# Filtered columns for five of six row components of a 3x3 convolution, with two sums moved from VectorE to accumulating DMAs

## The chip, the cores and the metric

One core of a Trainium2 chip runs the whole kernel. A core has TensorE (PE: matrix products; weight loads are its own row, PEld), VectorE (DVE), ScalarE (ACT), GpSimd (POOL) and SyncE (SP, which only issues transfers), with sixteen DMA engines. Each engine works through its own instructions in order, and engines wait for one another by semaphores. The metric is the device time of one launch in microseconds (us), as the median of several runs.

## The reference, cut to what matters

Two bottleneck blocks follow each other on an input x of 4 x 1024 x 56 x 56, all in float32. Layer 0 is a block with a deformable 3x3 convolution; layer 1 is a plain one with batch norms:

```python
out = relu(bn(conv(x, w1, b1), g1, be1))          # 1x1, 1024 -> 256
out = relu(bn(conv(out, w2, b2, pad=1), g2, be2)) # 3x3, 256 -> 256
out = bn(conv(out, w3, b3), g3, be3)              # 1x1, 256 -> 1024
out = relu(x + softplus(residual_scale)[0] * out)
```

`bn` takes the mean and the variance of each channel over all images and pixels. So nothing can be normalised before the whole convolution in front of it is done, and the kernel falls into stages at these points. The change lies in the 3x3 convolution of layer 1 and in what prepares and reads it. Its output before the batch norm is called y2.

## The kernel before, in words

**Stages.** Layer 0 runs from the start to about 2064 us. It also computes the first 1x1 convolution of layer 1 and stores that (y1) to DRAM. Then comes the 3x3 stage of layer 1 (to about 2378 us), a stage of second moments that gives the statistics of the last batch norm without computing its input (to about 2470 us), and the last stage, which computes the 1x1 convolution to 1024 channels, adds x and stores the output.

**The 3x3 stage.** An image of 56 rows is cut into two halves of 28 rows, so there are eight parts (`parts`). Within a part four output rows at a time are computed from six row components, p = 0 to 5, a fast convolution with four outputs along the rows; a part has QUADS = 7 such groups of four rows. Filters are transformed to the six components beforehand (`filters`, in layer 0), inputs are transformed on VectorE (`inputs`, lines 1150 to 1195), and the six products are turned back into four rows on VectorE (`end`, lines 1295 to 1333). The components are taken in the order `SEQ` = 1, 2, 3, 4, 0, 5. Each is first written into one of the four rows of its output (`TARGET`): components 0 and 1 into row class 0, component 2 into class 1, 3 into class 2, 4 and 5 into class 3.

Within a component, the three taps along a row are handled in one of two ways. Components in `WIN` have *filtered columns*: two neighbouring output columns come from four products (in `begin` one that goes to odd columns with the factor -2, in `middle` one that is added and copied to the even columns, in `end` one added to the odd and one subtracted from the even columns). The other components have five terms for a pair of columns. A term is 2 x 2 products of 128 x 128 filters (input and output channels are in two blocks of 128 each, `KB` = 2), with 7 x 28 = 196 columns, or 7 x 29 = 203 for one of the five. All go through `products`, line 1224.

For a filtered component ScalarE copies the odd columns out of the accumulator q (line 1238), and TensorE must wait for this copy before `middle` adds to q; then ScalarE copies the even columns (line 1262), and TensorE must wait for that before `end` adds to q again. The fourth product goes to a bank b of its own, and VectorE subtracts it (line 1278). Filters of filtered components need sums over the taps, `column_filters` (lines 772 to 781): components 2 and 4 get them in layer 0 (`EARLY`), component 5 at the start of the 3x3 stage (line 1401).

**Around the products.** `load(i)` brings the y1 rows of a part from DRAM into the place of the last image of y2 and ScalarE normalises them into the buffer d (line 1141). For a second half the row above it comes by a small transfer of its own into `edge`. `passes(i)` (line 1351) lets ScalarE read the finished rows of a middle part and sum values and squares for the batch norm: eight passes of 784 elements, two to each step of the loop. The first and last part (`ENDS`) use VectorE's statistics instead (line 1293).

**Order of the work.** The loop at line 1403 is written so that a component's `begin` stands ahead of the previous component's `end` and its own `middle` behind. A planner in the framework then orders the instructions of each engine by its own estimate of their times, so the order on the chip is near to, not equal to, that of the program. The transforms back of component 4 (`outer` and `inner`, lines 1303 to 1311) must be done before ScalarE may write component 5's odd columns, since both are in row class 3.

**Layer 0's filters.** `filters` (line 705) is a generator; the loop over the taps of the last image calls it once a tap. It loads the filters of layer 1, transforms them on VectorE, stores those of component 0 and their tap sum (`us_0`, in a buffer of the tag x1t that layer 0's last products also use) to DRAM, since their place is needed for the first rows of y1, and loads these.

**Reading y2.** y2 lies in SBUF, one tile for each image, rows in their order. The stage of moments reads it in runs of 128 pixels, the last stage in blocks of eight rows (`wide` line 1456, `sums_of_input` line 1637).

Of the kernel before, what the change touches and what calls it, by code (L numbers as in the profile page):

```python
# [8 lines left out]
F32 = mybir.dt.float32  # L9
# [22 lines left out]
WIN = (2, 4, 5)  # L32
EARLY = (2, 4)
# [28 lines left out]
def deform_bottleneck_then_bn_bottleneck(  # L62
# [27 lines left out]
    u0_d = dram.tile([128, KB * 3 * CB], F32, tag="u0_d", name="u0_d")  # L90
    y1_d = dram.tile([N, CB, HW], F32, tag="y1_d", name="y1_d")
# [81 lines left out]
    with ExitStack() as l0:  # L173
# [531 lines left out]
        def filters():  # L705
# [30 lines left out]
            def times(factor):  # L736
# [15 lines left out]
            nc.sync.dma_start(u0_d, w_0)  # L752
            us_0 = w3p.tile([128, 512], F32, tag="x1t", name="us_0", bufs=X1S)
            w_00 = w_0.rearrange("p (h j o) -> p h j o", h=KB, j=3)
            nc.vector.tensor_add(
                us_0.rearrange("p (h o) -> p h o", h=KB), w_00[:, :, 0], w_00[:, :, 1]
            )
            nc.sync.dma_start(us0_d, us_0)
            yield
# [7 lines left out]
            for p in (1, 3):  # L767
                us[p] = pool.tile([128, KB, CB], F32, tag=f"us{p}", name=f"us{p}")
                nc.vector.tensor_add(us[p], u[p][:, :, 0], u[p][:, :, 1])
                yield  # L770
# [12 lines left out]
        def raw_rows(to, n, half):  # L783

            lo = HALF * half
            for h in range(KB):
                nc.sync.dma_start(
                    to[:, h].rearrange("p r w -> p (r w)"),
                    y1_v[n, :, h, lo * W : (lo + HALF + 1 - half) * W],
                )  # L790
# [281 lines left out]

    with l1:
# [19 lines left out]
        nc.sync.dma_start(u[5], b_w2.rearrange("(h p) (i j) o -> i p h j o", p=128, j=3)[2])  # L1093
        for p in range(6):
            if p not in us:
                us[p] = wino.tile([128, KB, CB], F32, tag=f"us{p}", name=f"us{p}")
        nc.sync.dma_start(us[0], us0_d.rearrange("p (h o) -> p h o", h=KB))
        sum_t = wino.tile([128, KB, QUADS, W], F32, tag="sum_t", name="sum_t")
# [15 lines left out]
        edge = wino.tile([128, KB, W], F32, tag="edge", name="edge")  # L1114

        def load(i):

            n, half = parts[i]
            d = next_d if i else first_d
            pieces = []  # L1120
            if i == 0:
                for h in range(KB):
                    pieces.append((d[:, 1:, h, :], rows_t[:, h, : HALF + 1, :], h))
            else:
                lo = HALF * half
                land = y2[N - 1].rearrange("p h (r w) -> p h r w", w=W)[
                    :, :, lo : lo + HALF + 1 - half
                ]
                if half:
                    nc.sync.dma_start(edge, y1_v[n, :, :, (lo - 1) * W : lo * W])  # L1130
                raw_rows(land, n, half)
                for h in range(KB):
                    if half:
                        pieces.append((d[:, 0, h, :], edge[:, h], h))
                    pieces.append((d[:, 1 : 1 + HALF + 1 - half, h, :], land[:, h], h))
            nc.gpsimd.memset(d[:, HALF + 1 if half else 0], 0.0)
            for to, of, h in pieces:

                for e in range(2):
                    c = slice(e * (W // 2), (e + 1) * (W // 2))  # L1140
                    nc.scalar.activation(
                        to[..., c],
                        of[..., 1 - e : W : 2],
                        AF.Relu,
                        bias=sh1[:, h : h + 1],
                        scale=sc1[:, h : h + 1],
                    )
            return d

        def inputs(i, d, ps):  # L1150
# [5 lines left out]
            for hs in [slice(h, h + 1) for h in range(KB)] if i == 0 else [slice(0, KB)]:  # L1156
# [46 lines left out]
        def rows_of(n, half, r):  # L1203

            t = y2[n].rearrange("p o (r w) -> p o r w", w=W)
            r0 = HALF * half + r
            return t[:, :, r0 : r0 + 4 * (QUADS - 1) + 1 : 4, :]
# [10 lines left out]
        def products(ps, terms, first=False, last=False, alone=False):  # L1218

            for o in range(KB):  # L1220
                of = slice(o * 128, (o + 1) * 128)
                pairs = [(wt[:, h, of], x[:, :, h]) for h in range(KB) for wt, x in terms]
                for j, (wt, x) in enumerate(pairs):
                    nc.tensor.matmul(  # L1224
                        ps[:, o].rearrange("p r c -> p (r c)"),
                        wt,
                        x,
                        start=first and j == 0 and (alone or o == 0),
                        stop=last and j == len(pairs) - 1,
                        skip_group_check=not alone,  # L1230
                    )

        def begin(i, p):
# [13 lines left out]
            products(b, [(u[p][:, :, 1], x0)], first=True, last=True, alone=True)  # L1247
# [9 lines left out]

        def middle(i, p, q):
            if p in WIN:
                even, _ = halves(i, p)  # L1260
                products(q, [(u[p][:, :, 1], vs[p][..., :half_w])])
                nc.scalar.copy(even, q)

        def end(i, p, q):
# [7 lines left out]
            if p in WIN:  # L1272
                x0, x1 = v[p][..., :half_w], v[p][..., PW // 2 : PW // 2 + half_w]
                products(q, [(u[p][:, :, 2], x1)], last=True)
                b = bank(psb, "b", i, p, half_w)
                products(b, [(u[p][:, :, 0], x0)], first=True, last=True, alone=True)
                nc.vector.tensor_add(odd, odd, q)
                nc.vector.tensor_sub(even, even, b)
# [19 lines left out]
            elif p == 4:  # L1298
# [3 lines left out]

                def outer():
                    for o in range(KB):
                        stt(r[2][:, o], far_t[:, o], 4.0, sum_t[:, o], ALU.mult, ALU.add)
                    nc.vector.tensor_add(sum_t, sum_t, far_t)

                def inner(far):
                    for o in range(KB):
                        stt(far[:, o], r[3][:, o], 8.0, r[1][:, o], ALU.mult, ALU.add)  # L1310
                        stt(r[1][:, o], r[3][:, o], 2.0, r[1][:, o], ALU.mult, ALU.add)

                if i < len(parts) - 1:
                    outer()
                    inner(far_t)
                else:
                    inner(last_far)
# [4 lines left out]
            elif p == 0:  # L1322
                nc.vector.tensor_add(r[0], r[0], sum_t)
# [7 lines left out]
            elif p == 5:  # L1331
                nc.vector.tensor_add(r[3], r[3], far_t)
# [6 lines left out]
        CUTS = 2  # L1339
# [11 lines left out]
        def passes(i):  # L1351
            n, half = parts[i]
            size = HALF * W // CUTS
            for o in range(KB):
                for c in range(CUTS):
                    at = half * HALF * W + c * size
                    k = (i - 1) * CUTS + c
                    for f, func in enumerate((AF.Identity, AF.Square)):
                        nc.scalar.activation(
                            passed,  # L1360
                            y2[n][:, o, at : at + size],
# [34 lines left out]
        for ps in ((1, 2), (3, 4), (0,), (5,)):  # L1396
            inputs(0, ds[0], ps)
            for p in ps:
                if p in WIN and p not in EARLY:
                    for _ in column_filters(p):  # L1400
                        pass
        before, passing = None, iter(())
        for i, p in [(i, p) for i in range(len(parts)) for p in SEQ] + [(len(parts), None)]:
            begun = begin(i, p) if p is not None else None
            if before is not None:
# [9 lines left out]
                for _ in range(2):  # L1415
# [40 lines left out]
    def wide(n, j, k, name):  # L1456
        pz = ps1.tile([128, BLK], F32, tag="bank", name=f"{name}_{n}_{j}_{k}")
        for h in range(KB):
# [3 lines left out]
                y2[n][:, h, j * BLK : (j + 1) * BLK],  # L1462
# [174 lines left out]
    def sums_of_input(two):  # L1637

        (b11, b21), (b12, b22) = (
            [y2[n][:, h, j * BLK : (j + 1) * BLK] for h in range(KB)] for n, j in two  # L1640
# [3 lines left out]
        sub(t[:, 0], b12, b11)  # L1644
        sub(t[:, 1], b22, t[:, 0])
        sub(t[:, 2], b22, b12)
        sub(t[:, 3], b21, t[:, 1])
# [145 lines left out]
```

## Time and profile before

| | before |
|---|---|
| median of 3 runs | 2800.26 us (2799.1 to 2804.15) |
| the profiled execution | 2796.42 us, span 2794.6 us |
| granted TensorE clock, mean | 0.992 |
| line 1224 (all products of the 3x3 stage) | 1728 records, first at 2071.8, last ends at about 2372.4 us |
| line 1359 (statistics passes), ScalarE | 48 of 948 ns, and 48 of 187 ns that read the sum |
| line 1141 (normalising the rows), ScalarE | 32 of about 1.1 us, 16 of 0.4 us for the edge rows |
| POOL gathers of layer 0, line 509 | 900 of 1225 ns |

The page gives for each engine its busy time and share of the span, a chain of the work that ended last, and groups of instructions by source line. A line such as "L1238 ACT" is line 1238 of the kernel on ScalarE; "out<-in" names tiles. A table of stretches gives, for a window of time, each engine's busy time and number of instructions, then the granted clock, DMA share and GB/s.

### The profile page before, as it was taken

The numbers are of one execution on the slowest core, as the hardware profiler recorded it, in microseconds if no ns is written. First come the engines' busy times: TensorE is split into PE (matmuls) and PEld (weight loads), VectorE is DVE, ScalarE is ACT, GpSimd is POOL, SyncE is SP. The second block draws the span as 40 slices with busy tenths as digits, with TensorE's granted clock in tenths as the row PEclk, the third lists the DMA queues.
The fourth block names the chain that finished last, engine by engine and source line by source line (L and its number), as shares of the span: only waits on it lengthen the run. The fifth ranks groups of instructions, "written<-read, shape, count | busy, mean of one in ns | idle before, by whom it ended". The sixth has DMA issues, their size and how long they took to land.

```text
span 2794.6 us, 39694 instructions
## 1 busy us (share of the span) xinstructions
PE 2723.3 (97%) x12045; PEld 1928.1 (69%) x12045; DVE 2185.8 (78%) x5199; ACT 1496.3 (54%) x3045; POOL 1176.1 (42%) x1054
## 2 busy tenths in 40 slices
PE   9979999999999999999999999999989999999999
PEld 7655666776666676677667667667769999864554
DVE  5488887888788788877788888988759988337777
ACT  2345655575555655555565666666643444524444
POOL 0166554566655456556555656654500000111111
PEclk9999999999999999999999999999999999999999
DMA  8689999999999989999998999999831110219998
GB/s 286 200 300 368 389 324 339 328 349 339 341 335 363 349 296 317 328 351 348 352 349 269 362 370 333 340 343 375 268 123 31 42 39 9 95 53 343 349 346 303
DMA packets 313318, 792.70 MB, mean 284 GB/s; under 512 B 33768, under 2 KB 134672, under 8 KB 313104
## 3 DMA queue, kind: packets, MB, share of 16 engines
q0 software_dynamic: 127296, 462.48, 46.3%
q1 hardware_dynamic: 167376, 276.30, 28.7%
q10 hardware_dynamic: 18432, 51.39, 4.7%
q8 instruction: 95, 1.56, 0.2%
q14 instruction: 119, 0.97, 0.1%
HBM read 640.94 MB, written 143.75 MB: 281 GB/s over the span
## 4 chain that ended last, share of the span: by engine, by line
PE 81%; DMA 6%; DVE 6%; ACT 3%; issue 3%; SPq 1%; ACTq 0%; POOLq 0%; DVEq 0%
PE acc L574 20%; PE acc L662 11%; PE pr L636 10%; PE acc L331 8%; PE q L1224 6%; PE stp L546 6%; PE u L1674 3%; DMA g<-table,idxs 3%; PE acc_g L1506 2%; DVE s L521 2%; PE c L1674 2%; PE v L1674 2%; PE pm L421 2%; PE b L1224 2%; PE acc L868 1%
## 5 line engine op out<-in xcount | busy, mean ns | idle before, releaser
L509 POOL DMA_INDIRECT g<-table,idxs x900 | 1102.8, 1225 | 912.3 <-DVE s L521 244.3
L521 DVE SCALAR_TENSOR_TENSOR s<-g,wts,s 128x256 f32<-128x256 f32 (+1 forms) x2700 | 1173.4, 476 | 270.0 <-ACT s L519 130.0
L574 PE MATMUL acc<-sts,w 128*128 128x256 f32 (+2 forms) x3528 | 721.0, 355 | 2.8 <-ACT sts L552 1.4
L574 PEld LDWEIGHTS acc<-sts,w 128*128 128x128 f32 x3528 | 601.8, 190 | 54.1 <-ACT sts L552 4.3
L519 ACT ACTIVATE s<-g,wts 128x256 f32<-128x256 f32 x900 | 425.3, 511 | 213.7 <-PE stp L546 87.6
L636 PE MATMUL pr<-r,w 128*128 128x512 f32 (+2 forms) x896 | 365.8, 545 | 7.4 <-ACT r L609 4.0
L662 PE MATMUL acc<-x1t,c1w 128*128 128x512 f32 (+2 forms) x896 | 357.4, 541 | 7.5 <-ACT acc L283 4.2
L546 PEld LDWEIGHTS stp<-ident,s 128*128 128x128 f32 (+1 forms) x1800 | 211.5, 141 | 133.5 <-issue 92.0
L331 PE MATMUL acc<-xt,w 128*128 128x448 f32 x704 | 283.1, 544 | 6.7 <-DMA xt<-in_x_dram 6.7
L662 PEld LDWEIGHTS acc<-x1t,c1w 128*128 128x128 f32 x896 | 167.3, 190 | 146.6 <-issue 93.3
L636 PEld LDWEIGHTS pr<-r,w 128*128 128x128 f32 x896 | 165.0, 192 | 139.5 <-issue 84.3
L546 PE MATMUL stp<-ident,s 128*128 128x128 f32 (+1 forms) x1800 | 249.0, 273 | 10.2 <-DVE s L521 6.5
L552 ACT COPY sts<-stp 128x512 f32<-128x512 f32 (+2 forms) x504 | 241.1, 528 | 21.3 <-PE stp L546 21.0
L647 ACT ACTIVATE x1t<-pr,ch 128x512 f32<-128x512 f32 (+2 forms) x224 | 141.8, 633 | 139.8 <-PE pr L636 117.1
L331 PEld LDWEIGHTS acc<-xt,w 128*128 128x128 f32 x704 | 131.8, 192 | 111.1 <-issue 108.5
L1625 ACT ACTIVATE x1f<-x1f,sh_bn 128x896 f32<-128x896 f32 x112 | 116.0, 1041 | 150.2 <-DVE x1f L1622 129.6
L672 ACT COPY y<-acc 128x512 f32<-128x512 f32 (+2 forms) x112 | 59.5, 531 | 223.7 <-PE acc L662 212.1
L556 DVE TENSOR_TENSOR sts<-sts 128x512 f32<-128x512 f32 (+2 forms) x252 | 155.1, 615 | 0.8
L632 ACT COPY pr<-xr 128x512 f32<-128x512 f32 (+2 forms) x224 | 121.5, 542 | 3.8
L1622 DVE SCALAR_TENSOR_TENSOR x1f<-u,sc_bn,x1f 128x448 f32<-128x448 f32 x156 | 106.6, 683 | 18.9 <-PE u L1674 9.4
L1224 PE MATMUL q<-v,u 128*128 128x196 f32 x576 | 109.8, 338 | 8.4 <-DVE v L1176 7.7
L554 DVE TENSOR_TENSOR sts<-sts 128x256 f32<-128x256 f32 (+2 forms) x252 | 97.2, 386 | 23.4 <-ACT sts L552 22.0
(298 smaller groups left out, 3053.8 us busy)
## 6 DMA issues: line engine op xcount, KB each, us to landing
xt<-in_x_dram SPq DMA_DIRECT2D x112, 448.0 KB
x1f<-x_d SPq DMA_DIRECT2D x96, 448.0 KB
out_dram<-x1f ACTq DMA_DIRECT2D x96, 448.0 KB
xr<-in_x_dram SPq DMA_DIRECT2D x128, 256.0 KB
x_d<-x1t SPq DMA_DIRECT2D x128, 256.0 KB
table<-ft SPq DMA_DIRECT2D x56, 384.0 KB
g<-table,idxs POOLq DMA_INDIRECT x900
xr<-in_x_dram SPq DMA_DIRECT2D x64, 192.0 KB
```

Of the source, the lines that this page charges most:

```text
L331: nc.tensor.matmul(acc, w1[:, k, h * 128 : (h + 1) * 128], xts[n, j, k - k % 2][:, k % 2, :], start=start, stop=(k == KC - 1), skip_group_ ...
L509: nc.gpsimd.indirect_dma_start(out=g[:m], out_offset=None, in_=tables[n].rearrange("r q c -> r (q c)"), in_offset=bass.IndirectOffsetOnAxi ...
L519: nc.scalar.activation(s[:m], g[:m, 0:CB], AF.Copy, scale=wt[:, 0])
L521: nc.vector.scalar_tensor_tensor(s[:m], g[:m, corner * CB : (corner + 1) * CB], wt[:, corner], s[:m], ALU.mult, ALU.add,)
L546: nc.tensor.transpose(banks[h][:, t * 128 : t * 128 + m], s[:m, h * 128 : (h + 1) * 128], ident[:m, :m],)
L552: nc.scalar.copy(to, banks[h][:, :size].rearrange("p (e q) -> p e q", e=2))
L556: nc.vector.tensor_sub(sts[:, 5:7, :half], sts[:, 1:4:2, :half], sts[:, 0:2, :half])
L574: nc.tensor.matmul(sums[i], w2[:, a, k], sts[:, b, :half], start=(k == 0 and i % 2 == 0), stop=(k == TAPS - 1), skip_group_check=True,)
L636: nc.tensor.matmul(z, w3[:, h, k * 128 : (k + 1) * 128], r2[:, h, :size], start=False, stop=(h == KB - 1), skip_group_check=True,)
L662: nc.tensor.matmul(z, c1w[:, k, h * 128 : (h + 1) * 128], x1ts[k], start=False, stop=(i == KC // 2 - 1), skip_group_check=True,)
L1224: nc.tensor.matmul(ps[:, o].rearrange("p r c -> p (r c)"), wt, x, start=first and j == 0 and (alone or o == 0), stop=last and j == len(pai ...
L1674: nc.tensor.matmul(to, wt, x, start=start, stop=stop, skip_group_check=True)
```

## The change

- `WIN` becomes (0, 2, 3, 4, 5): components 0 and 3 get filtered columns too. `EARLY` becomes (2, 3, 4).
- In the middle parts (and in the last, but for its component 5) the even columns of a filtered component go another way. In `middle` ScalarE writes -q into a fresh bank b (a *seed*) instead of copying q to the even columns; in `end` TensorE adds the fourth product onto this bank, and ScalarE writes -b to the even columns. VectorE has no subtraction there.
- y2 is stored by row class: within an image, rows 0, 4, 8, ... come first, then rows 1, 5, 9, ..., and so on (`classes`). The four rows of a part are then contiguous, and VectorE's sums in the transform back take both channel blocks in one instruction (`joined`). Readers that need eight rows in order use `block_rows`.
- The two last sums of a middle part (row class 0 plus `sum_t`, row class 3 plus `far_t`) are transfers that add to their target, issued by GpSimd (`onto`); in the first and last part VectorE still does them.
- Statistics passes are cut by row class: sixteen of 392 elements a part, three to a step.
- The row above a second half is loaded together with its rows; `edge` goes.
- The tap sums of the filters of component 5 move to layer 0, with those of components 0 and 3, and go through DRAM as component 0's do (`u5_d`, `us5_d`).
- In part 0 only the inputs of components 1 and 2 are done one channel block at a time.

```diff
-WIN = (2, 4, 5)
-EARLY = (2, 4)
+WIN = (0, 2, 3, 4, 5)
+EARLY = (2, 3, 4)
...
-            nc.sync.dma_start(u0_d, w_0)
-            us_0 = w3p.tile([128, 512], F32, tag="x1t", name="us_0", bufs=X1S)
...
-            nc.sync.dma_start(us0_d, us_0)
-            yield
+            for p, w_p, u_d, us_d in ((0, w_0, u0_d, us0_d), (5, w_2, u5_d, us5_d)):
+                us_p = w3p.tile([128, 512], F32, tag="x1t", name=f"us_{p}", bufs=X1S)
+                u[p] = w_p.rearrange("p (h j o) -> p h j o", h=KB, j=3)
+                us[p] = us_p.rearrange("p (h o) -> p h o", h=KB)
+                yield from column_filters(p)
+                nc.sync.dma_start(u_d, w_p)
+                nc.sync.dma_start(us_d, us_p)
+                yield
...
+    def classes(t):
+        return t.rearrange("p o (c q w) -> p o c q w", c=4, w=W)
+
+    def block_rows(n, h, j):
+        return classes(y2[n])[:, h, :, 2 * j : 2 * j + 2, :].rearrange("p c q w -> p q c w")
...
-            for hs in [slice(h, h + 1) for h in range(KB)] if i == 0 else [slice(0, KB)]:
+            by_h = (i, ps) == (0, (1, 2))
+            for hs in [slice(h, h + 1) for h in range(KB)] if by_h else [slice(0, KB)]:
...
         def rows_of(n, half, r):
-            t = y2[n].rearrange("p o (r w) -> p o r w", w=W)
-            r0 = HALF * half + r
-            return t[:, :, r0 : r0 + 4 * (QUADS - 1) + 1 : 4, :]
+            return classes(y2[n])[:, :, r, QUADS * half : QUADS * (half + 1), :]
...
+        def seeded(i, p):
+            return i > 0 and (i, p) != (len(parts) - 1, SEQ[-1])
+
         def middle(i, p, q):
             if p in WIN:
                 even, _ = halves(i, p)
                 products(q, [(u[p][:, :, 1], vs[p][..., :half_w])])
-                nc.scalar.copy(even, q)
+                if seeded(i, p):
+                    seeds[i, p] = bank(psb, "b", i, p, half_w)
+                    nc.scalar.activation(seeds[i, p], q, AF.Copy, scale=-1.0)
+                else:
+                    nc.scalar.copy(even, q)
+
+        def onto(i, to, t):
+            if i in ENDS:
+                nc.vector.tensor_add(to, to, t)
+            else:
+                nc.gpsimd.dma_start(to, t, accum_op=ALU.add)
...
                 products(q, [(u[p][:, :, 2], x1)], last=True)
-                b = bank(psb, "b", i, p, half_w)
-                products(b, [(u[p][:, :, 0], x0)], first=True, last=True, alone=True)
-                nc.vector.tensor_add(odd, odd, q)
-                nc.vector.tensor_sub(even, even, b)
+                if seeded(i, p):
+                    b = seeds.pop((i, p))
+                    products(b, [(u[p][:, :, 0], x0)], last=True)
+                    nc.vector.tensor_add(odd, odd, q)
+                    nc.scalar.activation(even, b, AF.Copy, scale=-1.0)
+                else:
...
                 def outer():
-                    for o in range(KB):
-                        stt(r[2][:, o], far_t[:, o], 4.0, sum_t[:, o], ALU.mult, ALU.add)
-                    nc.vector.tensor_add(sum_t, sum_t, far_t)
+                    stt(r2, f_t, 4.0, s_t, ALU.mult, ALU.add)
+                    nc.vector.tensor_add(s_t, s_t, f_t)
...
-                    inner(far_t)
+                    inner()
+                    stt(f_t, r3, 6.0, r1, ALU.mult, ALU.add)
...
-                nc.vector.tensor_add(r[0], r[0], sum_t)
+                onto(i, joined(r[0]), joined(sum_t))
...
-                nc.vector.tensor_add(r[3], r[3], far_t)
+                onto(i, joined(r[3]), joined(far_t))
...
-        CUTS = 2
+        CUTS = 4
...
-                for _ in range(2):
+                for _ in range(3):
                     next(passing, None)
...
-                y2[n][:, h, j * BLK : (j + 1) * BLK],
+                block_rows(n, h, j),
```

## The prediction

> **What bounds the kernel now.** I read the page first, then the table of stretches, the groups by line and the waits of the 3x3 stage, its chain of waits, and last the timeline around one row component.
>
> ```profile
> span 2794.6 us, 39694 instructions
> PE 2723.3 (97%) x12045; PEld 1928.1 (69%) x12045; DVE 2185.8 (78%) x5199; ACT 1496.3 (54%) x3045; POOL 1176.1 (42%) x1054
> ```
>
> TensorE is busy for 97% of the span, so work taken off it can count, wherever no other engine sets the pace. The change is in the 3x3 stage of layer 1, from about 2072 to 2374 us. The stretches of that stage (columns: length, then busy time and instructions of PE, weight loads, VectorE, ScalarE, GpSimd, then clock, DMA share, GB/s):
>
> ```profile
> 2072.00:2160.00 88.00, 87.81 (x502) 86.80 (x503) 86.90 (x156) 26.74 (x52) 1.12 (x8) 0.97 0.16 58
> 2160.00:2350.00 190.00, 189.18 (x1102) 184.80 (x1102) 166.86 (x251) 96.75 (x188) 2.61 (x19) 1.00 0.11 36
> ```
>
> Two things are to be seen. TensorE is full in both. VectorE is full too up to 2160 (86.9 of 88 us), and after that has 12% left (166.9 of 190). ScalarE has half its time left, DMA nearly all. A part (half an image, eight in all) now takes 300.4 us (first to last product, 2071.8 to 2372.2) / 8 = 37.6 us.
>
> What a product costs, from the chain of waits in one part (start, length, engine, tile, line, records; each 128x128 product leaves two records):
>
> ```profile
> 2210.28 1.38 PE b L1224 x8
> 2211.65 1.36 PE q L1224 x8
> ```
>
> Four products of 203 columns take 1.38 us, four of 196 take 1.36 or 1.34. From the timeline of part 0, VectorE as TensorE comes to row 5's second product (line 1311 is the last operation that row 5's first copy waits for):
>
> ```profile
> 2111.36 1.02 DVE L1310 SCALAR_TENSOR_TENSOR far_t<-y 128x392 f32<-128x392 f32 x2
> 2112.30 1.03 DVE L1311 SCALAR_TENSOR_TENSOR y<-y 128x392 f32<-128x392 f32 x2
> 2113.26 1.02 DVE L1293 BATCH_NORM_STATS2 y_stats<-y 128x6 f32<-128x392 f32 x2
> 2114.20 0.95 DVE L1177 SCALAR_TENSOR_TENSOR v<-vs,v 128x784 f32<-128x784 f32 x1
> ```
>
> Starts that follow without a gap give the cadence: 0.885 us for 784 elements, 0.475 for 392.
>
> And ScalarE's hand on TensorE, from the queries on line 1262 (the first three) and line 1238 (the last two): who waited for these copies, us and times:
>
> ```profile
>   PEld q L1224: 4.2, 13
>   DVE y L1278: 1.0, 3
>   PE q L1224: 0.5, 2
>   PEld q L1224: 1.8, 6
>   PE q L1224: 0.2, 1
> ```
>
> **The change, part by part.**
>
> *Products.* A row without filtered columns has five terms, 20 products a part (4 of them 203 wide); one with them has four, 16 products of 196. Rows 0 and 3 change over: 2 rows x 8 parts x 1.38 us = **-22.1 us** on TensorE. A part goes from 37.6 to about 34.8 us.
>
> *VectorE, middle parts* (1 to 6). Inputs: rows 0 and 3 trade one 406-element operation (0.49) for two of 392 and one of 784 (1.835): +1.345 each, +2.69. Begin and end: rows 0 and 3 go from two 392-element operations to one, rows 2, 4, 5 also from two to one, because ScalarE now subtracts: 5 x -0.475 = -2.38. The joined sums: three pairs of 392 become three of 784, 3 x -0.065 = -0.2. The two sums that become DMAs: -1.77. Net -1.65 on 166.86/190 x 37.6 = 33.0, so 31.4 us for 34.8 us of TensorE. VectorE stays second there, at 90%.
>
> *VectorE, start and part 0*, where it is already full. Stage start: row 5's filter sums leave (cadence 0.60 + 0.60 + 0.33 + 0.60 = -2.1), rows 3 and 4 done whole +0.6, row 0 +1.1, row 5 -0.4: -0.8. Part 0 has neither seeds nor DMAs: +2.69 - 0.2 = +2.5. So VectorE reaches line 1311 of part 0 where it does now, about 2113, while TensorE has 2 x 1.38 us less to do before it; part 1 repeats this. What TensorE saves in parts 0 and 1, 2 x 2.76 = 5.5 us, is therefore not had: **+5.5**. The ends: +2 if TensorE runs further ahead into part 1 while row 5 waits (it has 8 products of row 1 to fill with), +9 if VectorE's extra 2.5 us comes on top.
>
> *ScalarE.* A filtered row now takes three ScalarE steps (odd columns, seed, even columns; 0.41 us each by cadence) instead of two, in five rows instead of three. Two of them stop TensorE: the odd copy before the second product, the seed before the third and fourth. Before, the fourth was free to be put anywhere; now it waits for its seed. Today's 48 copies hold the weight loads up 6.0 us and the products 0.7. For 80 such copies: 6.0 x 80/48 = 10.0, **+4.0**. Ends: 0.7 x 80/48 = 1.2, +0.5 (loads run ahead of the products, so not all of it reaches them); three steps in five rows, 6.0 x 120/48 = 15, +9. The statistics passes go from 8 of 0.95 + 0.19 us to 16 of about 0.53 + 0.19, some 2 us more a part; the edge copies (4 x 0.4 us on every other part) go. ScalarE comes to some 21 of 34.8 us, but in order: behind a pass that waits stand the next row's odd copy and seed, and for these waits TensorE.
>
> *The two DMAs a part* (12 in all). Each is issued by POOL behind ScalarE's even and VectorE's odd columns. Behind it on POOL stands only the clearing of one column of v (0.12 us), for which VectorE's difference waits. The profile has no transfer within SBUF, nor an adding one. The nearest row for the issue is line 509, 1225 ns a gather, so 1.2 us; for the data the first hardware queue: 28.7% of 16 x 2794.6 us over 167,376 packets is 77 ns for a packet of 1.65 KB. Here 256 runs of 1568 B over 16 engines: 16 x 77 ns = 1.2 us, doubled for reading the target, 2.5 us. The Trainium skill ("DMA: Bandwidth & Descriptors", anatomy of one DMA) states a fixed 2.0 us besides bytes over 436 GB/s; with 401 KB that is an estimated 2.9, and with the issue 4.1. Row and fixed part together: 1.2 + 2.5 + 2 = 5.7 us. The first pass comes after the second product of row 5, row 1's twelve and row 5's last eight: 24 x 0.34 = 8.2 us, and the pass over row 3's class is the seventh, two row steps later. So **0**, hidden behind 8.2 us of products; without that cover 5.7 us of ScalarE twice a part.
>
> A rule that speaks against it: the same skill's "SBUF — State Buffer" (section "two separate sides", the "DVE blocks DMA" trap) says that POOL, writing descriptors, is shut out of a port pair that certain VectorE operations hold for their whole length. The row is line 509, which ran beside a VectorE 78% busy at 1.2 us mean, up to about 3 us in the timeline. By the row the sum is unchanged; by the rule, at 3 us, landing is 7.5 us, still inside 8.2 but with nothing left. I go by the row and keep the rule for the slow rival.
>
> *Layer 0.* Ten more small VectorE operations (0.6 or 0.33 us, 5.4 in all) and two stores (1.0 MB, at 350 GB/s 3 us of DMA) while the gathers hold DMA above 90%; SP issues the first rows' load behind them, which ran at 1899 us, needed at 2066, so it has room. The second sum tile takes one of six x1t buffers for a few taps. TensorE is full there and has other blocks' work to turn to: **+2**, between 0 and 6.
>
> *Tail and last stage.* In part 7 the end is VectorE's (line 1299 at 2364.0 to the statistics at 2377), so row 0's saving there, 1.38, is lost; one 0.475 operation and a little more go: **+0.8**. Products on the blocks of 8 rows read four runs of 56; line 1224 reads runs of 28 at full rate, so 0. GpSimd's four differences (1.14 us each) have 20 us of products over them.
>
> Sum: -22.1 + 5.5 + 4.0 + 0 + 2 + 0.8 = **-9.8 us**. The profiled execution took 2796.4 (span 2794.6 and 1.8 around it), 3.8 below the median of the runs, 2800.3. So 2786.6 for a profiled one, and **2790** on the scale of the median.
>
> **Rivals.**
>
> *Everything fills up.* The order of TensorE's work is planned, and now loses under 1 us in 190. With +2, +0.5 and 0 for layer 0: -22.1 + 2 + 0.5 + 0.8 = -18.8, 2781. For it: the spare 12% of VectorE. Against: VectorE at 99% to 2160.
>
> *Saving eaten on the spot.* VectorE +9, ScalarE +9, layer 0 +2, tail 0.8: -1.3, 2799. For it: ScalarE already runs 7 us without a gap (passes between line 1141's copies, 2270 to 2277) and TensorE waited there.
>
> *Slower: passes stuck behind the adding DMA.* If landing takes longer than the 8.2 us of cover, ScalarE stands still in front of a pass, odd copy and seed behind it, and TensorE has some 4 products (1.4 us) in hand. Each part then loses landing less 9.6. It takes 9.8 + 5.6 = 15.4 us over six parts, 2.6 each, to be slower: a landing of 12.2 us. At 15 us: 6 x 5.4 = 32, 2822. For it: gathers of up to 11.4 us stand in the chain of layer 0. Against: these are under a DMA share of 0.9 and more, here it is 0.11.
>
> **How the numbers follow.** Forecast 0.42 (2785 to 2794); everything fills 0.17; eaten 0.18; slower 0.23. 0.2% is 5.6 us, about what a measurement here tells from no change. Faster 0.58, same 0.18, slower 0.24. The range leaves out the best tail and most of the slow rival's upper half: 2779 to 2812.
>
> **What would show it.** Right: 1600 records of line 1224 instead of 1728, from first to last about 288 us; VectorE full until some 2150 with TensorE gaps only there; passes that start without waiting on a DMA. Wrong: TensorE gaps in every part, before products that wait on the seed or odd copy (then ScalarE was mis-sized), or with a pass waiting for the DMA ahead of them (then the landing).

## The result, and the profile after

The changed kernel takes 2814.69 us (median of 12 runs, 2803.99 to 2820.12) beside 2798.45 us for the kernel before (12 runs, 2794.54 to 2804.15): ratio 1.0051, 95% interval 1.0037 to 1.0066. It is slower by some 14 us by the ratio (16 between the two medians), where 2790 was forecast; the range given ended at 2812. Run again beside later experiments it came to 1.0048 (1.0030 to 1.0067).

The profiled execution took 2820.12 us, at the top of those 12; another, 12 us shorter, has the same 3x3 stage (313.0 and 314.4 us). So only the stage is compared below, and not the spans. First the page of the kernel after:

```profile
span 2818.0 us, 39650 instructions
PE 2716.3 (96%) x11917; PEld 1912.8 (68%) x11917; DVE 2182.4 (77%) x5152; ACT 1520.3 (54%) x3159; POOL 1192.4 (42%) x1080
```

TensorE has 128 records of products fewer (11917 for 12045), as the change says, and lower busy time, yet the span grew. So TensorE waits somewhere. The table of stretches of the kernel after, with windows that answer to the two shown of before (this stage starts 6 us later here), the whole stage, and 8 us of part 0 (columns as before: length, then busy time of PE, weight loads, VectorE, ScalarE, GpSimd, then clock, DMA share, GB/s):

```profile
2078.00:2166.00 88.00, 82.17 (x454) 80.20 (x455) 83.68 (x129) 24.09 (x45) 2.74 (x12) 0.94 0.19 65
2166.00:2356.00 190.00, 172.64 (x979) 164.79 (x979) 157.18 (x215) 112.52 (x270) 15.99 (x39) 0.99 0.23 56
...
2077.90:2390.90 313.00, 285.14 (x1600) 273.00 (x1600) 261.05 (x374) 155.83 (x366) 20.22 (x56) 0.98 0.20 54
...
2122.00:2130.00 8.00, 6.41 (x20) 5.89 (x21) 8.00 (x14) 1.79 (x5) 0.19 (x1) 0.57 0.01 2
```

The same stage of the kernel before:

```profile
2071.80:2372.20 300.40, 299.24 (x1731) 293.38 (x1732) 269.00 (x437) 132.62 (x259) 3.90 (x30) 0.99 0.12 40
```

Before, TensorE was busy for 299.2 of 300.4 us of this stage. Now it is busy for 285.1 of 313.0: it lost 1.2 us to idling then and loses 27.9 now, along the whole stage, while no other engine is full after 2166 (VectorE 83%, ScalarE 59%). Waits set the pace there, and not an amount of work.

The chain of waits of the kernel after, where part 2 goes over into part 3, shows two of them (start, length, engine or transfer, tile, line):

```profile
2196.04 0.48 DVE y L1296
...
2197.06 4.38 DMA y<-sum_t
...
2201.46 0.03 ACT y L1254
...
2202.85 0.39 ACT y L1297
2203.24 0.60 ACT passed L1385 x2
2203.84 0.18 issue
2204.02 4.40 DMA y<-far_t
...
2208.54 0.58 DVE y L1309
2209.12 0.04 issue
2209.17 5.12 PE q L1227 x28
2214.29 1.35 PE b L1227 x8
```

Both adding transfers stand in the chain, one behind the other, 4.4 us each from GpSimd's start to landing. What waits for the first is line 1254, row 1's odd copy *of the next part* (row 1 is component 1, as in the prediction). It writes other rows, in another half of the image, than the transfer touches. A product group costs 1.35 us as before, so the size of the term "products" was right.

Who waited for these transfers in the whole kernel after (waiter, us, times; from the query on the issuing line 1280):

```profile
L1280 POOL DMA_DIRECT2D y<-sum_t x6: 1197/1200/1317, 2161.4 to 2353.3; - x6
L1280 POOL DMA_DIRECT2D y<-far_t x6: 1197/1202/1220, 2167.5 to 2360.3; - x6
...
  ACT y L1254: 14.9, 3
  DVE y L1296: 6.6, 5
  ACT passed L1385: 5.6, 2
  ACT y L1241: 3.1, 1
  DVE y L1309: 3.1, 3
```

Six of each kind ran, but line 1254 waited three times, about 5 us each: in front of parts 3, 5 and 7, the second halves, whose y2 tile is the one that the transfer adds to. In front of parts 2, 4 and 6, which write another image's tile, the planner put it ahead of the transfer (in part 4 it started at 2232.56 us, the transfer at 2237.19), and it never waited for one. The statistics passes (line 1385), the only waiters that the prediction had looked at, account for 5.6 us.

And who waited for ScalarE's copies in the kernel after, the seed (line 1272, first two lines) and the odd copy (line 1241, last two), to set against 4.2, 0.5, 1.8 and 0.2 us before:

```profile
  PEld q L1227: 13.5, 23
  PE q L1227: 6.8, 12
...
  PEld q L1227: 8.3, 8
  PE q L1227: 5.8, 6
```

TensorE itself now stands 12.6 us in front of products that wait for one of these two, where it stood 0.7. Last, TensorE in part 0 of the kernel after, from its timeline (the brackets hold the idle time before and who ended it; eight records are 1.5 us at full clock):

```profile
2117.72 1.63 PE L1227 MATMUL q<-v,u 128*128 128x196 f32 x8 [2.69 <-ACT y L1274]
2119.19 1.49 PE L1227 MATMUL q<-vs,u 128*128 128x196 f32 x8
2122.66 2.80 PE L1227 MATMUL q<-vs,us 128*128 128x196 f32 x8 [1.98 <-DVE y L1301]
2126.39 2.98 PE L1227 MATMUL q<-v,u 128*128 128x196 f32 x8 [0.93 <-ACT y L1274]
```

Three gaps, 5.6 us, and two groups at half clock, with the granted clock at 0.57 in the 8 us shown above. Line 1274 is the even copy of the rows without seeds, and VectorE was busy through all of it. The chain there has this:

```profile
2116.17 0.89 DVE far_t L1339
...
2117.16 0.52 ACT y L1274
...
2117.72 2.97 PE q L1227 x16
```

Row 0's even copy writes row class 0 and waits for the last of VectorE's operations behind row 4 (line 1339), which touches classes 1 and 3.

### The profile page after: what moved, and what is told of

Read it like the earlier page. It is cut to its first block, busy times and chain, and to the rows that moved or that the text cites. A ratio compares the mean times of both kernels' runs of the same rounds, so it can differ in the third digit from the quotient of the medians.

```text
span 2818.0 us, 39650 instructions
## 1 busy us (share of the span) xinstructions
PE 2716.3 (96%) x11917; PEld 1912.8 (68%) x11917; DVE 2182.4 (77%) x5152; ACT 1520.3 (54%) x3159; POOL 1192.4 (42%) x1080
## 4 chain that ended last, share of the span: by engine, by line
PE 79%; DVE 7%; DMA 6%; ACT 4%; issue 3%; SPq 1%; another core or an unknown queue 0%; ACTq 0%; DVEq 0%; POOLq 0%
PE acc L576 21%; PE acc L664 12%; PE pr L638 11%; PE acc L333 8%; PE stp L548 6%; PE u L1697 3%; PE q L1227 3%; PE acc_g L1528 2%; PE c L1697 2%; PE v L1697 2%; PE pm L423 2%; DVE s L523 2%; DMA g<-table,idxs 1%; DMA y<-sum_t 1%; PE acc L869 1%
## 5 line engine op out<-in xcount | busy, mean ns | idle before, releaser
L1227 PE MATMUL q<-v,u 128*128 128x196 f32 x448 | 90.7, 347 | 18.8 <-DVE v L1178 7.4
```

The lines of the kernel that those rows point to most:

```text
L1227: nc.tensor.matmul(ps[:, o].rearrange("p r c -> p (r c)"), wt, x, start=first and j == 0 and o == 0, stop=last and j == len(pairs) - 1, sk ...
```

## The experiments

**The theory** after these readings: a copy or sum on a y2 tile waits for any unfinished operation on the same tile whose addresses reach across it, even where the bytes are others. The two channel blocks of a tile lie 3136 elements apart, so an operation on both blocks spans 3528 of the tile's 6272 elements, and any two such spans overlap. A slow adding transfer then holds up all that follows on its image, and a seed, which goes to a bank of its own, is held up by none of it. **Rivals**: the loss is ScalarE's (80 seeds and copies on an engine that works in order); or the transfers hurt by the passes behind them; or layer 0 gives the time away. All times of a stage below are from first to last product in one profile; two profiles of the kernel after gave 313.0 and 314.4, so 1 to 2 us tell nothing.

**Both sums back on VectorE.**

```diff
         def onto(i, to, t):
-            if i in ENDS:
-                nc.vector.tensor_add(to, to, t)
-            else:
-                nc.gpsimd.dma_start(to, t, accum_op=ALU.add)
+            nc.vector.tensor_add(to, to, t)
```

> The changed kernel with the two last sums of a middle part done by VectorE instead of the adding DMAs; all else as changed. Theory A (the DMAs' landing stands on the path, because operations on other bytes of the same image wait for it): TensorE's three gaps of 1.5 to 2.0 us at the second half of each image go (10.3 us in all), nobody waits on a DMA, VectorE takes 1.77 us a part more but stays under TensorE; about 2803 us. Theory B (ScalarE's three steps a row are what stops TensorE): the gaps in front of products that wait for the seed stay and the time stays within 4 us of the changed kernel's 2814.7. Theory C (VectorE is the bound): slower than the changed kernel, by up to 6 x 1.77 = 10.6 us.

Measured: 2792.41 us, ratio 1.0003 (0.9993 to 1.0013): level with the kernel before. The stage takes 301.5 us, 11.5 below the kernel after, although VectorE has 8.4 us more to do in it (269.4 for 261.1). The stretch of that stage in this variant:

```profile
2068.30:2369.80 301.50, 284.94 (x1600) 274.89 (x1600) 269.43 (x386) 156.89 (x366) 5.62 (x44) 0.97 0.12 41
```

So without the transfers the rest of the change comes out level. TensorE's waits agree with this price. In the kernel after it stood 4.6 us in front of products that waited for row 1's copy (line 1254) and 3.9 for VectorE's sum of that row (line 1309); both are gone here, and its waits for the seed (line 1272) went from 6.8 to 4.2 us: 11.1 us in all. Those for the odd copies (line 1241) stayed, 5.8 and then 5.6 us:

```profile
PE q L1227 <- ACT y L1241: 5.6, 4, 1.9
PE q L1227 <- ACT b L1272: 4.2, 5, 2.8
```

But TensorE still idles 16.6 us here, and part 0's gaps stay (2.61, 1.98 and 1.09 us). The rest of the saving of 22.1 us is lost elsewhere.

**No seeds anywhere.**

```diff
         def seeded(i, p):
-            return i > 0 and (i, p) != (len(parts) - 1, SEQ[-1])
+            return False
```

> The changed kernel without seeds: ScalarE copies q to the even columns and VectorE subtracts the fourth product, as for the filtered rows before the change; DMAs as changed. Theory A: the gaps that wait for the DMAs stay, about 10 us; only the gaps in front of a seed (6.8 us) can go, and VectorE is fuller by 5 x 0.475 us a part; 2808 to 2815. Theory B: the 10.8 us of gaps that wait on ScalarE go; about 2804. Theory C: slower, by up to 6 x 2.4 = 14 us.

Measured: 2827.16 us, ratio 1.0138 (1.0123 to 1.0153), stage 331.1 us, 18 more than the kernel after. So ScalarE's amount of work is not what costs: it has 13.6 us less to do (142.2 for 155.8) and all is slower. What the third step of a row costs by itself this run can't say, since its even copies get waits of their own. The waits of this variant's stage say why:

```profile
ACT y L1274 <- DMA y<-sum_t: 42.4, 6, 10.8
ACT y L1274 <- DVE far_t L1339: 42.4, 7, 13.9
```

Without seeds the even copies go to y2, and each stands behind a transfer or VectorE's chain on the same tile. A seed goes to a bank and has no such wait.

**Channel blocks side by side.** If the spans are to blame, storing the two blocks' elements alternately should free row classes and halves from one another, since a row class of a part is then one run of addresses.

```diff
     def classes(t):
-        return t.rearrange("p o (c q w) -> p o c q w", c=4, w=W)
+        return t.rearrange("p h x -> p (h x)").rearrange(
+            "p (c q w o) -> p o c q w", c=4, o=KB, w=W
+        )
```

(`sum_t`, `far_t` and all readers likewise.) Once with the transfers, once with both sums on VectorE:

> The changed kernel with another order of y2 in SBUF: row class, then rows, then columns, with the two channel blocks innermost, so that the bytes of one row class of one half are one run and the span of addresses of no part's rows crosses that of another. Seeds, DMAs and passes as changed. Theory A: only passes and the next part's first use of the sum tiles wait for a DMA, the gaps at second halves go (10.3 us), and the even copy of component 0 in part 0 no longer waits for the sums of component 4 (2.7 us and the half clock behind it); 2797 to 2803. Theory B and C: no change, within 4 us of 2814.7. Reading every second element may cost something in the last stage, which then is longer than 419 us.

> Both: the order of y2 with no crossing spans, and VectorE's sums instead of DMAs. Theory A: within 4 us of the run with the order of y2 alone, since a DMA that only passes wait for costs nothing; VectorE's 1.77 us a part may show as a few us. Theory C: slower than the run with the order of y2 alone by up to 10 us.

Measured: 2818.55 us, ratio 1.0103 (1.0089 to 1.0117), stage 315.7; and 2807.87 us, ratio 1.0068 (1.0047 to 1.0088), stage 309.2. As a time this says little, since the layout brings a cost of its own: ScalarE writes every fourth element, and that is slow. The odd copy of this variant with the transfers, and then the same copy of the kernel after (min, median and max in ns):

```profile
L1249 ACT ACTIVATE y<-q x40: 839/887/942, 2074.2 to 2376.7; 128x392 f32<-128x392 f32 x40
```

```profile
L1241 ACT ACTIVATE y<-q x40: 501/526/540, 2085.9 to 2386.7; 128x392 f32<-128x392 f32 x40
```

ScalarE grew by 34 us in the stage (189.6 for 155.8). As a reading of waits it is clear: of all operations only the passes still wait for a transfer between 2100 and 2360 us.

```profile
ACT passed L1392 <- DMA y<-sum_t: 11.6, 4, 3.9
```

The waits of row 1's copy and of VectorE's adds are gone with the overlap of the addresses. In part this is so because the planner now puts row 1's odd copies ahead of the transfers (at 2182.24 us against 2188.08 in front of part 3). But that transfer landed 5.5 us after it began, and in between row 1's even copies (at 2188.77) and VectorE's adds (at 2189.79 and 2191.44) ran on the same tile without waiting for it. That settles why the waits were there. It doesn't settle a price: here the transfers cost 6.5 us of stage, and how much of it is passes standing in ScalarE's queue isn't separated.

**Seeds in part 0, and transfers in odd parts only.** Three variants: `seeded` without its `i > 0`, with both sums on VectorE; the same with transfers in parts 1, 3 and 5 alone, behind which another image's tile comes; the same with all twelve.

```diff
         def seeded(i, p):
-            return i > 0 and (i, p) != (len(parts) - 1, SEQ[-1])
+            return (i, p) != (len(parts) - 1, SEQ[-1])
...
         def onto(i, to, t):
-            if i in ENDS:
+            if i in ENDS or parts[i][1] == 0:
```

These three leave out a part of the sum in part 0, by all signs that of rows 2 to 4: by the order of the banks their seeds lie where no product of this stage had yet written. The Trainium skill ("PSUM — Partial Sum Buffer", The four PSUM rules) says that ScalarE's writes don't mark a bank as written, and that a product that isn't flagged as the first of a group overwrites where the mark is clear; that fits, and no run here takes it apart. Number and form of the instructions are those of the full work.

> The variant whose two sums stay on VectorE, with one thing more: part 0 takes the seeds too, so that no even copy of part 0 goes into y2 before the row ends. In that variant part 0 lost 2.61 + 1.98 + 1.09 us of TensorE to idle gaps and some 2.6 us more to two groups of products at half clock. If the gaps come from the even copies that stand behind VectorE, about 6 to 8 us go: stage of the 3x3 near 294 us, ratio to the kernel before about 0.998. Rival: part 0 is set by VectorE's amount of work, and only the five subtractions that leave it (5 x 0.475 = 2.4 us) come back: stage near 299, ratio about 0.9995.

> Seeds in part 0 too, and the two sums as adding DMAs only in parts 1, 3 and 5, where the next part writes another image's tile; VectorE adds in parts 2, 4 and 6. If what made the DMAs dear is that later operations on the same image's tile wait for them, six DMAs of the twelve are free here: the time is that of the variant with seeds in part 0 and all sums on VectorE, or up to 3 us below it, since 3 x 2 x 0.885 us of VectorE go. If DMAs are dear wherever they stand (the passes behind them, the ports), half of the 11.5 us come back: some 6 us above that variant.

> The changed kernel with seeds in part 0 too, all twelve DMAs kept. The two losses are separate places, so they should add: the DMAs' loss (11.5 us by the stage of the variant without them) stays, part 0's goes. If part 0 is worth 6 to 8 us, ratio to the kernel before about 1.002 to 1.003; if 2.4, about 1.004. If both losses have one cause, this run is level with the variant without DMAs, 0.998.

| sums | ratio to before | stage |
|---|---|---|
| all on VectorE | 0.9987 (0.9974 to 1.0001) | 297.0 us |
| transfers in parts 1, 3, 5 | 0.9990 (0.9974 to 1.0007) | 295.9 us |
| transfers in parts 1 to 6 | 1.0048 (1.0027 to 1.0069) | 310.8 us |

This is the clearest of the experiments. Six transfers behind which the next part writes another tile cost nothing, net of the sums that VectorE no longer does; the other six cost 14.9 us of stage (310.8 less 295.9). In both the passes stand behind transfers. The waits on transfers from 2100 to 2360 us with those in odd parts only, and then those of the variant with all, from 2090 to 2350 us:

```profile
ACT passed L1385 <- DMA y<-sum_t: 5.2, 2, 2.6
ACT y L1297 <- DMA y<-sum_t: 4.7, 1, 4.7
DVE y L1296 <- DMA y<-sum_t: 1.9, 3, 0.9
```

```profile
ACT y L1254 <- DMA y<-sum_t: 17.8, 3, 6.5
DVE y L1296 <- DMA y<-sum_t: 7.8, 5, 2.8
ACT passed L1385 <- DMA y<-sum_t: 5.9, 2, 3.2
ACT y L1297 <- DMA y<-sum_t: 4.7, 1, 4.7
ACT y L1241 <- DMA y<-far_t: 3.1, 1, 3.1
DVE y L1309 <- DMA y<-far_t: 3.1, 3, 1.0
```

ScalarE waits in its passes nearly as long in the first as in the second (5.2 and 5.9 us), and the first loses nothing by it: the cover that the prediction counted on for the passes is there. What the second has besides is above all row 1's copy, three waits of some 6 us, and that has no cover. The seeds in part 0 bring 4.5 us of stage (301.5 to 297.0) with the sums on VectorE, between the 2.4 of the rival and the 6 to 8 expected, so how much of it is waits and how much is VectorE's lighter work stays open; and 2 to 4 with the transfers (313.0 and 314.4 to 310.8), which its ratio does not tell from nothing.

**Layer 0's part alone.** The kernel before, with row 5's filter sums moved to layer 0 and nothing else.

```diff
-            nc.sync.dma_start(u0_d, w_0)
-            us_0 = w3p.tile([128, 512], F32, tag="x1t", name="us_0", bufs=X1S)
...
+            for p, w_p, u_d, us_d in ((0, w_0, u0_d, us0_d), (5, w_2, u5_d, us5_d)):
...
-        nc.sync.dma_start(u[5], b_w2.rearrange("(h p) (i j) o -> i p h j o", p=128, j=3)[2])
+        nc.sync.dma_start(u[5], u5_d.rearrange("p (h j o) -> p h j o", h=KB, j=3))
```

> The kernel before with one part of the change alone: row 5's filter sums and its column filters are made and stored in layer 0, and the start of the 3x3 stage loads them. By the prediction's terms, +2 us in layer 0 and about -2 at the start of the stage: level, ratio 1.000. If layer 0 has no room for the ten operations and two stores: up to +6, ratio 1.002. If it hides them entirely, -2 us, ratio 0.9993.

Measured: 2797.49 us, ratio 1.0000 (0.9988 to 1.0012), stage 299.3 us for 300.4. Level. This run moves four of the ten small operations and both stores. The rest of layer 0's share was not run alone, but the variant with both sums on VectorE has all of it, and its whole is behind the kernel before by 0.8 us (ratio 1.0003), no more than its stage is (1.1 us). Layer 0 gives nothing away that shows.

**Row 5 released earlier.** In the variant with seeds and all sums on VectorE, TensorE's longest waits are for row 5's odd copy (line 1241), which stands behind the last operation of VectorE's chain after row 4, since that chain reads row class 3 to its end. The same sums can be made so that class 3 is free after two operations. Seeds in part 0 are kept for rows 0 and 5 alone, whose banks have been written in full by then. (The cut shows the new order alone; the sums are on VectorE, or in parts 1, 3 and 5 transfers, as above.)

```diff
-                nc.vector.tensor_add(far_t, r[2], r[3])
-                nc.vector.tensor_sub(r[3], r[2], r[3])
+                nc.vector.tensor_sub(far_t, r[2], r[3])
+                nc.vector.tensor_add(r[2], r[2], r[3])
...
-                    stt(r2, f_t, 4.0, s_t, ALU.mult, ALU.add)
-                    nc.vector.tensor_add(s_t, s_t, f_t)
+                    nc.vector.tensor_add(s_t, s_t, r2)
+                    stt(r2, r2, 3.0, s_t, ALU.mult, ALU.add)
...
-                    stt(r1, r3, 2.0, r1, ALU.mult, ALU.add)
+                    stt(r1, f_t, 2.0, r1, ALU.mult, ALU.add)
...
-                    stt(f_t, r3, 6.0, r1, ALU.mult, ALU.add)
+                    stt(f_t, f_t, 6.0, r1, ALU.mult, ALU.add)
...
```

> The changed kernel as it is, beside the next two on one chip: 1.005 to the kernel before, 3x3 stage 313 us, as first measured. It is the base from which the two others are read.

> Both sums on VectorE; in part 0 seeds for rows 0 and 5 alone (their banks have been written in full by then); and the same six operations behind row 4 in another order: the difference of row classes 2 and 3 goes into far_t, the sum stays in row class 2, so that row class 3 is read for the last time by the second operation and not by the sixth. Row 5's first copy, which writes row class 3, is then free 4 x 0.885 = 3.5 us earlier. In the variant with seeds in part 0 TensorE idled 8.5 us in front of products that waited for this copy (six gaps of 0.5 to 1.9), 2.8 us behind a row of passes that had piled up meanwhile, and lost some 3 us to half clock. If these are one cause, most of it goes: stage 287 to 291 us against 297, ratio to the kernel before about 0.996. Rival: VectorE's amount of work sets the pace, a wait only moves to the next product: stage 295 to 297, ratio 0.9985 to 0.9995.

> The same with the two sums as adding DMAs in parts 1, 3 and 5 alone, where no operation on the same tile follows. If VectorE still sets the pace anywhere in these parts, 1 to 3 us less than the variant before; if not, level with it. Slower by 3 or more would say that the DMAs cost also where nothing of the next part waits for them.

| kernel | median | ratio to before | stage |
|---|---|---|---|
| after, again | 2807.51 us | 1.0048 (1.0030 to 1.0067) | 314.4 us |
| earlier release | 2786.66 us | 0.9972 (0.9958 to 0.9985) | 295.5 us |
| the same, transfers in parts 1, 3, 5 | 2786.51 us | 0.9968 (0.9958 to 0.9979) | 294.8 us |

Both beat the kernel before, by some 8 us, and the kernel after by some 21. They are level with each other: relieving VectorE of six sums brings nothing that shows. But the reason given for the earlier release was mostly wrong. The stage fell by 1.5 us, not by 6 to 10; the ratio moved from 0.9987 to 0.9972, and the two intervals overlap. TensorE's waits in front of line 1241 went from 8.5 us to 6.2, and those in front of the seed (line 1272) rose from 4.4 to 6.7. Part 0 also has three seeds fewer than in that variant, and its gap in front of line 1241 grew from 1.9 to 3.2 us; the three large ones of the later parts fell from 5.2 to 2.1 in all. So the copy did come free earlier there, and most of the gain went to the seeds: the wait moved, as the rival had it. Here is where to, from ScalarE and then TensorE in this variant's part 6:

```profile
2299.90 4.12 ACT L1142 ACTIVATE rows<-y,sh_bn,sc_bn 128x812 f32<-128x812 f32 x4
2303.91 0.48 ACT L1272 ACTIVATE b<-q 128x392 f32<-128x392 f32 x1
```

```profile
2304.45 2.98 PE L1227 MATMUL q<-v,u 128*128 128x196 f32 x8 [3.57 <-ACT b L1272]
```

Four normalisations of the next part's rows, 4.1 us in one block, stand ahead of a seed that TensorE waits for, and the four products behind it (eight records) ran at half clock, 2.98 us for 1.49. Cutting that block was not tried.

## Why the prediction was wrong, point by point

- **The two DMAs a part: "0, hidden behind 8.2 us of products".** This step failed, and it turned the sign. Its own numbers held: 1.2 us for the issue (measured 1.20, at most 1.32, so a lock-out by VectorE does not show), and landing, put at 5.7 us, or 4.1 by its other estimate, took 4.4. (The gathers of line 509 that it went by took up to 5.69 us, and not about 3; that misreading did no harm.) What was wrong is who waits. Only the passes were asked about, and they do have cover. Everything else that is written to the same image afterwards was not: row 1's copy of the next part above all, in three of six transitions, with two landings in series. Price by the runs: 11.5 us of stage for all twelve, set against the relief of VectorE, and 14.9 for the six that matter.
- **Products, -22.1.** Right: 1600 records for 1728, groups still 1.34 to 1.36 us. The busy time of TensorE fell by only 14.1 us (299.2 to 285.1), since a group behind a gap takes longer (1.59 or 1.63 in place of 1.49) and some ran at half clock.
- **VectorE in the middle parts.** Right: 7.9 us less in the whole stage (269.0 to 261.1), where its terms up to part 6 give 6 x -1.65 - 0.8 + 2.5 = -8.2.
- **VectorE in part 0, +5.5.** The place was right, the mechanism incomplete. It was taken that TensorE would not gain there. In fact it stops: the even copies of the rows without seeds wait behind VectorE's chain on other row classes. Seeds in part 0 took 4.5 us of this away, up to 2.4 of it perhaps by five subtractions fewer on VectorE.
- **ScalarE, +4.0 (0.5 to 9).** This step failed too: it was too small, and its cause another. With the transfers gone TensorE's products stood 9.8 us in front of seeds and odd copies (4.2 and 5.6, shown above), 9.1 more than before: over twice the term, at its upper bound. Its weight loads, which the estimate was scaled from, stood 18.6 us (9.8 and 8.8) where 10.0 was estimated. The estimate scaled the old wait by the number of steps. What costs is order: row 5's copy stands behind VectorE's chain after row 4, ScalarE idles meanwhile (22.5 us in five waits in the kernel after), its passes pile up, and a later seed stands behind them and the normalised rows.
- **Layer 0, +2.** Nothing shows: ratio 1.0000 (0.9988 to 1.0012) with row 5's share of it alone.
- **Tail, +0.8.** Right: from the last product of the stage to the first transpose of the next, 7.9 us for 7.1.
- **Half clock after short gaps** was in no term. In the first profile of the kernel after it lost some 3.4 us (0.43 of the 8 us in part 0).
- **The rival with the right sign**, passes stuck behind the adding transfer, was right that ScalarE would stand still with a copy behind it, and wrong in its threshold of 12.2 us: 4.4 us were enough, since the copy itself waits and the count of 8.2 us of products doesn't apply to it. "Saving eaten on the spot" at 2799 is near the variant with both sums on VectorE (1.0003); for the kernel after it is wrong.

Of the sum: predicted for the stage, from first to last product, -22.1 + 5.5 + 4.0 = -12.6 (the 288 us of the prediction), measured +12.6. Of the 25.2 between, the transfers are 11.5 (one edit, measured). The other 13.7 are what the variant without them loses beyond the prediction; that alone would have made the change level and not 10 us faster, so the transfers explain why it is slower and not all of the error. Against a stage that only saved its products (300.4 - 22.1 = 278.3) this variant loses 23.2 us where the prediction had 9.5: 15.4 more of idling than before (16.6 less 1.2), and 7.8 in product groups that run longer behind gaps or at half clock (busy 284.9, for 299.2 - 22.1 = 277.1). The gaps of its timeline are part 0's 5.7 us, 5.1 in front of row 5's odd copy and 2.8 in front of one seed, and smaller ones. Seeds in part 0 gave 4.5 of it back. How the rest divides is read from gaps and not shown by a run: the one that tried to take the second away (the earlier release) moved the wait.

## What to carry to other kernels

Before calling a transfer hidden, list every later operation on the *same tile*, in the next iteration too, and not only the reader that needs its bytes: a dependence may be kept by the span of addresses, and then a tile with two blocks far apart makes neighbours of everything in it. Put slow asynchronous work where the next thing done is on another tile; here that made six transfers free and six cost 15 us. When an engine is relieved but waits set the pace, ask first what releases the next copy, since shortening one wait mostly hands it on to the next in the same queue.

## What the runs showed of the hardware that was not expected

- Gaps of 2 to 3 us on TensorE can halve its clock: after idle times of 2.69, 1.98 and 0.93 us within 12 us, four products (eight records) took 2.98 us instead of 1.49, and the granted clock of 8 us was 0.57. It isn't regular: the second profile of the kernel after had gaps of 3.14 and 2.13 us at the same place, one group of 2.26 us, the next of 2.57, and then full clock; and in the first profile groups behind gaps of 1.95 and 1.96 us took 1.59 us.
- An SBUF to SBUF transfer of 392 KB that adds to its target landed 4.4 us after GpSimd began to issue it, 1.2 us of that the issue, in a stage with a DMA share of 0.20.
- ScalarE's copy of 392 elements out of a bank took 526 ns when it wrote every second element, and 887 ns when it wrote every fourth.
